# Soft-disc attention layer: norm-factor products in pairs, exponentials one step earlier, output units regrouped, value copies on VectorE

## The chip, the cores and the metric

One NeuronCore of a Trainium2 chip runs the whole program. The metric is device time in microseconds, the median of several executions. Engines are named as the profile names them: PE (matrix products), PEld (its weight loads), DVE (vector), ACT (activation functions), POOL (GpSimd), SP (which only issues DMAs here).

## The reference

Four layers act one after the other on a tensor of 8 images x 32 x 32 tokens x 256 channels in f32, each as `x = x + layer(groupnorm(x))`. The change lies in the last one, layer 3, a local attention with a soft disc as its window:

```
qkv = silu(x @ w_qkv.T);  q, k, v = split(qkv)                  # 8 heads of 32 channels
q, k = rope(rms_norm(q, w_qn)), rope(rms_norm(k, w_kn))         # norm over the 32 channels
wp = silu(x @ w_wp.T + b_wp);  width_raw, sharp_raw = split(wp) # one pair per token and head
width = sigmoid(width_raw) * sqrt(2) * 3 + 0.5
sharp = sigmoid(sharp_raw) * 9.5 + 0.5
mask = sigmoid((width - rel_dist) * sharp)                      # over the 7 x 7 neighbours
attn = softmax(scores / sqrt(32) - (1 - mask) * 10000)
out = rms_norm(attn @ v_window, w_on)                           # norm over all 256 channels
return silu((out + v) @ w_out.T)
```

The position that the rotary embedding sees is the head's, not the token's: q and k of a head are turned by the same angles, which cancel in the scores, so the kernel has no work for it.

## The kernel before, in words

Channels lie on the 128 partitions, in two chunks c of four heads each. Layer 3 works in 128 groups of 128 query tokens: image b (8), chunk c (2), pair of blocks t (8). A chunk number J = 2b + c stands for eight groups, so an image is 16 steps.

**The loop.** The order on PE, ACT, DVE and POOL is written by hand (`manual_schedule`): each engine executes what is emitted for it in exactly the order of emission, and waits at its head instruction for what this needs. SP is free of that order, but also works its own queue from the front. At step n the loop emits `scores(n+3)` (16 small products into four PSUM tiles `s`), `exps(n)` (four exponentials on ACT with row sums `su`), the planned units due at n, `logits(n+3)` (four reductions on DVE, which free the `s` tiles), the first half of `turn(n-2)` (transposes `pt` on PE, copied to `pts` by DVE), `finish()`, `soft(n+5)` (four tanh on ACT, the soft mask), `divide(n)` (reciprocal on DVE, multiply on POOL), the units due at n + 0.5, the second half of `turn(n-2)`, `finish()` again, `values(n-3)` (products `o`, copied into `oT` by DVE) and `masked(n+5)` (an addition on POOL).

**The units.** `Fillers` holds (due time, unit) pairs; those that are due are emitted in order of time, and of entry where times agree. A unit emits its products and often its ACT instruction at once and returns the rest (DVE, POOL, DMA) as a function, which goes into the list `later` and is emitted by the next `finish()`. For a chunk that starts at step n = 8J the plan has: `project` for k and q at n - 12 to n - 10.5 and for v at n - 7.5 and n - 7 (two products over 512 tokens, `qkv_ps`, L2015; a tanh `th`, L2000; the rest on DVE, with squares for q and k on POOL), `roots` at n - 8 (sums of squares by products into `ms_ps`, Ln and Exp on ACT, L2110 and L2111, which need another activation table and so a table load before and one after), four `head_scale` at n - 6 to n - 4.5 (a product of 32 rows with the norm factors, `fac_ps`, L2117, and a multiply on DVE, L2121), `in_strips` (POOL), and five `vturn` units (four transposes `vt` and a copy to `v` on ACT, L1744). Per image there are the group norm, `normed` (two ACT instructions), two `discs` units (products `wp_ps`, then a chain DVE, ACT, DVE, ACT, DVE that makes width and sharpness, L2055 to L2067), and the tail: squares of `oT`, a share in a later `roots`, four `tail_scale` (a product with the weights `won` on one row of factors, L2150, a multiply, an addition of v on POOL), and four `output` units (two products `out_ps` each, tanh, DVE, POOL, store) with a `reload` of the residual `xr` three steps ahead of each.

**Buffers.** All PSUM tiles come from one ring of eight banks, so a product can start only when the tile eight places back has been read. One step takes nine or ten of them. `xr` has three buffers, `su` four, `fac` two; the masks and probabilities live in nine fixed tiles.

**Where roots fall.** `roots` for J falls on step 8J - 8, that is on steps 0 and 8 of every image period of 16. In this text half A is the stretch from the roots at step 0 (odd J) to those at step 8, and half B the other. Images' tails come two images later: in steady state an output unit falls on steps 1.5, 7, 7.5 and 9.5, a tail product on steps 14 to 15.5.

Of the kernel before, what the change touches and what calls it, by code (L numbers as in the profile page):

```python
# [16 lines left out]
P = 128  # L17
# [15 lines left out]
def shape_constants():  # L33
# [55 lines left out]
    ).astype(f)  # L89
    k["k_spread"] = (p[:, None] % 32 == p[None] // 32).astype(f)  # L90
    return {n: np.ascontiguousarray(v) for n, v in k.items()}

# [13 lines left out]
def layouts(inputs):  # L106
# [38 lines left out]
    )  # L145
    a["l3_on"] = i["L3_conv_w_on"].reshape(2, P)
    a.update(shape_constants())
# [204 lines left out]
class First3(First):  # L352
# [8 lines left out]
    def early(self):  # L361
# [25 lines left out]
        def factors():  # L387
            won, spread = self.won, self.spread
            nc.vector.tensor_scalar(self.bwp, self.bwp, 0.5, None, ALU.mult)
            nc.gpsimd.tensor_scalar(self.wo, self.wo, 0.5, None, ALU.mult)  # L390
            nc.vector.tensor_mul(won[:, 0], won[:, 0], won[:, 1])
            nc.vector.scalar_tensor_tensor(
                spread[:, 0], won[:, 0], -(32.0**-0.5) / MASK_SCALE, spread[:, 0],
                ALU.mult, ALU.mult,
            )
            nc.vector.memset(won, 0.0)

        def weight():
            for h in range(2):
                nc.sync.dma_start(  # L400
                    self.won[32 * h + 8 : 32 * h + 9], a["l3_on"].unsqueeze(0)
                )

# [1230 lines left out]
class DiscStream(Stream):  # L1634
# [8 lines left out]
    def __init__(self, K, wk, cp, pp, pairs, n_img, ebufs):  # L1643
        super().__init__(K, wk, pp, pairs, n_img, ebufs)
        self.slots, self.s = 20, {}
        shape = [P, 4, 2 * self.PART]
        self.tiles = [cp.tile(shape, F32, name=f"e{i}") for i in range(ebufs)]
# [36 lines left out]
    def exps(self, n):  # L1684
        mx, e = self.mx.pop(n), self.prob(n)
        self.su = self.wk.tile([P, 4], F32, name="su", bufs=4)
        for j in range(4):
            self.nc.scalar.activation(  # L1688
                e[:, j], e[:, j], AF.Exp, scale=-1.0, bias=mx[:, j : j + 1],
                accum_out=self.su[:, j : j + 1],  # L1690
            )

    def divide(self, n):
        e = self.prob(n)
        self.nc.vector.reciprocal(self.su, self.su)  # L1695
        self.nc.gpsimd.tensor_mul(e, e, self.su.unsqueeze(2).to_broadcast([P, 4, NWIN]))  # L1696

# [37 lines left out]
    def value_unit(self, strips, dst, u):  # L1735
        ps = self.ring("vt")
        for i in range(4):
            col, r = divmod(4 * u + i, 5)
            self.nc.tensor.transpose(
                ps[: self.PART, i * P : i * P + P],  # L1740
                strips[:, col, 8 * r : 8 * r + 8].rearrange("p i j -> p (i j)"),
                self.K.ident,
            )
        self.nc.scalar.copy(  # L1744
            dst[: self.PART, 4 * u : 4 * u + 4, :],
            ps[: self.PART, :].rearrange("p (s c) -> p s c", c=P),
        )
# [202 lines left out]
def layer3(tc, K, src, dst, n_img, a, first):  # L1950
    nc = tc.nc
    pairs = disc_pairs()
    with tc.tile_pool(name="l3c", bufs=1, reuse_waits="tile") as cp, tc.tile_pool(
# [16 lines left out]
        K.ring = st.ring  # L1970
        bwp, sel, spread, won = first.bwp, first.sel, first.spread, first.won
        wo, win, eps = first.wo, first.win, first.eps
# [68 lines left out]
        def discs(b, u):  # L2041
# [11 lines left out]
            def rest():  # L2053
# [4 lines left out]
                )  # L2058
                th = wk.tile([P, 4, 16], F32, name="dth")
                nc.scalar.activation(th, d, AF.Tanh)  # L2060
                nc.vector.scalar_tensor_tensor(d, th, 1.0, d, ALU.add, ALU.mult)
                nc.scalar.activation(d, d, AF.Tanh, scale=0.5)
                wd, sp = d[:, :, 0:8], d[:, :, 8:16]
                md = math.sqrt(2.0) * 3
# [48 lines left out]

        def head_scale(J, s, h):
            g = slice(32 * (2 * s + h), 32 * (2 * s + h) + 32)
            ps = st.ring("fac_ps")
            nc.tensor.matmul(ps, spread[g, s], fac[J][g], start=True, stop=True)  # L2117

            def rest():
                d = dest(J, s, h)  # L2120
                nc.vector.tensor_mul(d, d, part(ps))  # L2121

            return rest
# [12 lines left out]
        def vturn(J, u):  # L2136
            b, c = divmod(J, 2)
            if u == 0:
                st.v[b, c] = wk.tile([P, st.slots, P], F32, name="v", bufs=2)
            st.value_unit(strips, st.v[b, c], u)  # L2140

# [4 lines left out]

        def tail_scale(J, b, c, h):
            g, hs = slice(32 * h, 32 * h + 32), slice(h * HALF, (h + 1) * HALF)
            ps = st.ring("fac_ps")
            nc.tensor.matmul(ps, won[g, c], fac[J][g], start=True, stop=True)  # L2150

            def rest():
                d = st.o[b, c][:, hs]
                nc.vector.tensor_mul(d, d, ps)
                nc.gpsimd.tensor_add(d, d, vT[b, c][:, hs])

# [28 lines left out]
        def plan_chunk(J):  # L2185
# [4 lines left out]
            for i in range(4):  # L2190
                s, h = 1 - i // 2, i % 2
                fill.add(n - 12 + i / 2, lambda s=s, h=h: project(J, s, h))
                fill.add(n - 6 + i / 2, lambda s=s, h=h: head_scale(J, s, h))
            fill.add(n - 7.5, lambda: project(J, 2, 0))
            fill.add(n - 7, lambda: project(J, 2, 1))
            fill.add(n - 6, lambda: in_strips(J))

        def plan_image(b):
            n = 16 * b
            if b:  # L2200
# [8 lines left out]
                for c in range(2):  # L2209
                    fill.add(n - 13.5 + c / 2, lambda c=c: normed(b, c))  # L2210
                for u in range(2):
                    fill.add(n - 10 + u / 2, lambda u=u: discs(b, u))
            for c in range(2):
                fill.add(n + 19 + c, lambda c=c: tail_sq(b, c))
                for h in range(2):
                    fill.add(
                        n + 30 + c + h / 2,
                        lambda c=c, h=h: tail_scale(2 * b + 4, b, c, h),
                    )
            for i in range(4):  # L2220
                at = n + 32 + (1.5, 7, 7.5, 9.5)[i]
                fill.add(at - 3, lambda i=i: reload(b, i // 2, i % 2))
                fill.add(at, lambda i=i: output(b, i // 2, i % 2))

        for J in range(2 * n_img + 3):
            b, c = divmod(J, 2)
            t = b - 2 if c == 0 and b >= 2 else None
            if J and (J < 2 * n_img or t is not None):
                fill.add(8 * J - 8, lambda J=J, t=t: roots(J, t))
            if J < 2 * n_img:  # L2230
                plan_chunk(J)
        for b in range(n_img):
# [14 lines left out]
        def finish():  # L2247
            while later:
                later.pop(0)()

        def start():

            units(-11)
            rest = [discs(0, 0), discs(0, 1), project(0, 1, 0)]
            rest[0]()
            rest[2]()
            r = project(0, 1, 1)
            rest[1]()
            r()
            soft(0)  # L2260
# [8 lines left out]
            in_strips(0)  # L2269
            for i in range(4):  # L2270
                head_scale(0, 1 - i // 2, i % 2)()
            masked(1)
# [6 lines left out]
        with tc.manual_schedule(engines={E.PE, E.Activation, E.DVE, E.Pool}):  # L2279
            start()  # L2280
            for n in range(-4, N + 3):
                if 0 <= n + 3 < N:
# [3 lines left out]
                    st.scores(n + 3)  # L2286
                if 0 <= n < N:
                    st.exps(n)
                units(n)
# [73 lines left out]
```

## Time and profile before

| | |
|---|---|
| median of three runs | 3330.1 us (3329.66 to 3331.37) |
| profiled execution | 3334.75 us, its span 3333.0 us |
| mean granted TensorE clock | 0.976 |
| busy share of the span | PE 96%, PEld 49%, DVE 66%, ACT 68%, POOL 45% |
| layer 3 | 2529 to 3333 us |
| transposes `pt` in it (L1706) | 1024 records, 164.7 us |
| projections `qkv_ps` (L2015) | 384 records, 191.4 us |
| norm-factor products (L2117) | 128 records, 81.7 us |
| tail products (L2150) | 64 records, 33.4 us |
| copies of v on ACT (L1744) | 80, 45.9 us |

The shares are means over four layers with different limits, so layer 3 has to be read from its own stretch. An f32 product of 512 columns shows as two records. Busy time is the time in which at least one instruction of the group was running; where records overlap, their mean duration times their number is more than that. The clock is what the throttle granted to PE, 1.00 being full speed.

### The profile page before, as it was taken

The numbers are of one execution on the slowest core, as the hardware profiler recorded it, in microseconds if no ns is written. First come the engines' busy times: TensorE is split into PE (matmuls) and PEld (weight loads), VectorE is DVE, ScalarE is ACT, GpSimd is POOL, SyncE is SP. The second block draws the span as 40 slices with busy tenths as digits, with TensorE's granted clock in tenths as the row PEclk, the third lists the DMA queues.
The fourth block names the chain that finished last, engine by engine and source line by source line (L and its number), as shares of the span: only waits on it lengthen the run. The fifth ranks groups of instructions, "written<-read, shape, count | busy, mean of one in ns | idle before, by whom it ended". The sixth has DMA issues, their size and how long they took to land. (4 is left out here: it accounts for less than half of the span.)

```text
span 3333.0 us, 77642 instructions
## 1 busy us (share of the span) xinstructions
PE 3203.6 (96%) x30792; PEld 1649.6 (49%) x30792; DVE 2185.0 (66%) x5570; ACT 2277.6 (68%) x5066; POOL 1491.7 (45%) x1073
## 2 busy tenths in 40 slices
PE   7999999999998999899999999999998999999997
PEld 3323323233232444667677766666664555555554
DVE  4776776777676667565555655666665667777775
ACT  3666666666676457755556547767676779888885
POOL 4233223323431011245444445344335658888777
PEclk9999999999999999999999999999998889999999
DMA  3000000000000666777787731111111001101001
GB/s 141 14 26 1 26 26 1 26 7 20 26 1 32 221 235 238 234 202 191 193 216 200 187 115 58 53 65 40 50 52 36 14 14 38 35 30 36 27 27 61
DMA packets 139183, 268.00 MB, mean 80 GB/s; under 512 B 9218, under 2 KB 77700, under 8 KB 130500
## 3 DMA queue, kind: packets, MB, share of 16 engines
q1 hardware_dynamic: 132436, 242.67, 24.3%
q10 hardware_dynamic: 6384, 20.37, 1.8%
q8 instruction: 243, 3.98, 0.5%
q14 instruction: 120, 0.98, 0.1%
HBM read 177.81 MB, written 85.20 MB: 79 GB/s over the span
## 5 line engine op out<-in xcount | busy, mean ns | idle before, releaser
L681 DVE TENSOR_TENSOR e<-s,ret 128x1024 f32<-128x1024 f32 x512 | 602.9, 1219 | 180.4 <-PE s L675 176.4
L685 ACT ACTIVATE ea<-e 128x1024 f32<-128x1024 f32 x512 | 535.1, 1055 | 267.8 <-DVE e L681 233.9
L675 PE MATMUL s<-qk,qk 32*128 32x512 f32 x2048 | 300.4, 640 | 2.4 <-POOL qk L567 1.7
L1564 POOL TENSOR_TENSOR e<-e,su 128x616 f32<-128x616 f32 (+2 forms) x128 | 157.3, 1229 | 269.8 <-DVE su L1563 240.2
L693 PE MATMUL sm<-ea,ones 128*32 128x512 f32 x2048 | 273.0, 604 | 2.0 <-DVE dn L701 2.0
L720 PE MATMUL num<-e,v 128*32 128x512 f32 x2048 | 266.6, 592 | 0.0
L1711 DVE COPY pts<-pt 112x512 f32<-112x512 f32 x256 | 175.9, 687 | 133.4 <-PE pt L1706 131.7
L2076 ACT ACTIVATE e<-win,disc 128x196 f32<-128x196 f32 x512 | 239.7, 544 | 0.3
L843 PE MATMUL up_ps<-x,wup 128*128 128x512 f32 x512 | 230.7, 605 | 3.2 <-POOL x L236 3.2
L1696 POOL TENSOR_TENSOR e<-e,su 128x784 f32<-128x784 f32 x128 | 191.3, 1495 | 82.7 <-DVE su L1695 53.9
L1688 ACT ACTIVATE e<-e,mx 128x196 f32<-128x196 f32 x512 | 228.0, 454 | 0.0
L2083 POOL TENSOR_TENSOR e<-e,win 128x784 f32<-128x784 f32 x128 | 201.7, 1576 | 37.8 <-issue 31.6
L1559 ACT ACTIVATE e<-e,mx 128x154 f32<-128x154 f32 (+2 forms) x512 | 212.3, 426 | 0.0
L1059 ACT ACTIVATE d<-d,cols 128x128 f32<-128x128 f32 x512 | 163.8, 392 | 67.9 <-POOL d L1050 67.8
L870 DVE SCALAR_TENSOR_TENSOR cv<-xm,par,cv 128x512 f32<-128x512 f32 x192 | 144.7, 754 | 85.5 <-ACT cv L865 80.9
L2015 PE MATMUL qkv_ps<-xq,w 128*128 128x512 f32 x384 | 191.4, 625 | 1.2 <-ACT fac L2110 1.2
L1255 POOL TENSOR_TENSOR decayed<-state,rb 128x520 f32<-128x520 f32 x48 | 50.8, 1058 | 304.7 <-PE sc L1188 112.5
L1796 PE MATMUL qkv_ps<-x,w 128*128 128x512 f32 x384 | 182.7, 613 | 1.6 <-POOL x L236 1.6
L1706 PEld LDWEIGHTS pt<-idg,e 128*112 128x112 f32 x1024 | 120.3, 139 | 120.5 <-issue 90.6
L675 PEld LDWEIGHTS s<-qk,qk 32*128 32x128 f32 x2048 | 85.3, 183 | 184.2 <-issue 120.4
L1706 PE MATMUL pt<-idg,e 128*112 128x128 f32 x1024 | 164.7, 287 | 8.4 <-DVE oT L1730 3.1
L1678 DVE CUSTOM_DVE_ANT_0 e<-s,e 128x196 f32<-128x196 f32 x512 | 153.7, 357 | 8.0 <-PE s L1665 4.2
(244 smaller groups left out, 6775.6 us busy)
## 6 DMA issues: line engine op xcount, KB each, us to landing
d<-l1rows SPq DMA_DIRECT2D x64, 512.0 KB
x<-x SPq DMA_DIRECT2D x25, 1024.0 KB
l1xm<-xm SPq DMA_DIRECT2D x16, 1024.0 KB
l1sz<-sz SPq DMA_DIRECT2D x16, 1024.0 KB
xv<-l1xm SPq DMA_DIRECT2D x32, 512.0 KB
l1xa<-xa SPq DMA_DIRECT2D x16, 1024.0 KB
xa<-l1xa SPq DMA_DIRECT2D x16, 1024.0 KB
rb<-l1rows SPq DMA_DIRECT2D x32, 512.0 KB
```

Source lines behind the costliest of these rows:

```text
L675: nc.tensor.matmul(s[:, j % 2], qk[b, 1, c][g, kb * P : (kb + 1) * P], qk[b, 0, c][g, h * HALF : (h + 1) * HALF], start=True, stop=True,)
L681: nc.vector.tensor_mul(e[n, i], s, m)
L685: nc.scalar.activation(ea[n, i], e[n, i], AF.Abs)
L693: nc.tensor.matmul(acc["sm"][g, :], ones, ea[n, j // 2][:, j % 2, :], start=kb == 0, stop=kb == 7,)
L720: nc.tensor.matmul(acc["num"][g, :], v[b][:, kb, vc], e[n, j // 2][:, j % 2, :], start=kb == 0, stop=kb == 7,)
L843: nc.tensor.matmul(ps, wup[:, kc, m * P : (m + 1) * P], seg(s)[:, kc], start=kc == 0, stop=kc == 1,)
L1559: self.nc.scalar.activation(p[:, j], p[:, j], AF.Exp, scale=-1.0, bias=mx[:, j : j + 1], accum_out=su[:, j : j + 1],)
L1688: self.nc.scalar.activation(e[:, j], e[:, j], AF.Exp, scale=-1.0, bias=mx[:, j : j + 1], accum_out=self.su[:, j : j + 1],)
L1706: self.nc.tensor.transpose(ps[: self.PART, at : at + P], self.tile(n)[:, 2 * i + j, k * self.PART : (k + 1) * self.PART], self.K.ident,)
L2015: nc.tensor.matmul(ps, w[:, kc, o : o + P], xq[b][:, kc, h * HALF : (h + 1) * HALF], start=kc == 0, stop=kc == 1,)
L2076: nc.scalar.activation(e[:, j], win[:, 0], AF.Tanh, scale=disc[b][:, i, 8 + h : 9 + h], bias=disc[b][:, i, h : h + 1],)
L2083: nc.gpsimd.tensor_add(e, e, win[:, 1].unsqueeze(1).to_broadcast([P, 4, NWIN]))
```

## The change

1. `head_scale` handles both token halves of q or of k in one unit: two products on two different groups of 32 rows stand next to each other on PE, with two PSUM tiles; the two multiplies follow together.
2. The tail's weight `w_on` moves out of the product: the product takes a matrix of ones on the factors' row, once for each token half instead of once for each half and channel chunk, and the weight, now a column per partition, is multiplied in by DVE in the same instruction as the factor.
3. `exps` is emitted one step earlier than `divide`, with `su` kept per group.
4. The copy of v out of PSUM is on DVE, in the next `finish()`, and no longer on ACT.
5. The chain of `discs` is cut into five pieces, one per `finish()`; `finish()` calls each function once and keeps what it returns for the next call.
6. The plan moves: v's two projections to n - 8.5 and n - 8 (the second is emitted just ahead of `roots`, which are entered later), `head_scale` to n - 6 and n - 5, `normed` from n - 13.5 to n - 15, `tail_scale` from n + 30 and later to n + 27.5 and n + 28.5 (n here an image's first step), the outputs from n + 33.5, 39, 39.5 and 41.5 to n + 29.5, 30.5, 31 and 31.5, in the order of token halves, with the reloads at n + 26.5 to n + 30.5.
7. Constants: a 128 x 128 matrix of ones on every row 8 of 32 is loaded in place of two rows of weights, and a memset before it goes.

```diff
         def weight():
-            for h in range(2):
-                nc.sync.dma_start(
-                    self.won[32 * h + 8 : 32 * h + 9], a["l3_on"].unsqueeze(0)
-                )
+            nc.sync.dma_start(self.won[:, 0], a["k_one8"])
+            nc.sync.dma_start(self.won[:, 1, 0:2], a["l3_on"])
...
-        self.nc.scalar.copy(
+        return lambda: self.nc.vector.tensor_copy(
             dst[: self.PART, 4 * u : 4 * u + 4, :],
...
-                th = wk.tile([P, 4, 16], F32, name="dth")
-                nc.scalar.activation(th, d, AF.Tanh)
+                return silu
+
+            def silu():
+                th = wk.tile([P, 4, 16], F32, name="dth", bufs=2)
+                nc.scalar.activation(th, disc[b][:, 4 * u : 4 * u + 4, :], AF.Tanh)
+                return lambda: silu2(th)
...
-        def head_scale(J, s, h):
-            g = slice(32 * (2 * s + h), 32 * (2 * s + h) + 32)
-            ps = st.ring("fac_ps")
-            nc.tensor.matmul(ps, spread[g, s], fac[J][g], start=True, stop=True)
+        def head_scale(J, s):
+            ps = [st.ring("fac_ps") for _ in range(2)]
+            for h in range(2):
+                g = slice(32 * (2 * s + h), 32 * (2 * s + h) + 32)
+                nc.tensor.matmul(ps[h], spread[g, s], fac[J][g], start=True, stop=True)
...
-        def tail_scale(J, b, c, h):
+        def tail_scale(J, b, h):
             g, hs = slice(32 * h, 32 * h + 32), slice(h * HALF, (h + 1) * HALF)
             ps = st.ring("fac_ps")
-            nc.tensor.matmul(ps, won[g, c], fac[J][g], start=True, stop=True)
+            nc.tensor.matmul(ps, ones[g], fac[J][g], start=True, stop=True)
 
             def rest():
-                d = st.o[b, c][:, hs]
-                nc.vector.tensor_mul(d, d, ps)
-                nc.gpsimd.tensor_add(d, d, vT[b, c][:, hs])
+                for c in range(2):
+                    d = st.o[b, c][:, hs]
+                    nc.vector.scalar_tensor_tensor(
+                        d, d, on[:, c : c + 1], ps, ALU.mult, ALU.mult
+                    )
+                    nc.gpsimd.tensor_add(d, d, vT[b, c][:, hs])
...
-                fill.add(n - 6 + i / 2, lambda s=s, h=h: head_scale(J, s, h))
-            fill.add(n - 7.5, lambda: project(J, 2, 0))
-            fill.add(n - 7, lambda: project(J, 2, 1))
+            for s in range(2):
+                fill.add(n - 5 - s, lambda s=s: head_scale(J, s))
+            fill.add(n - 8.5, lambda: project(J, 2, 0))
+            fill.add(n - 8, lambda: project(J, 2, 1))
...
-                    fill.add(n - 13.5 + c / 2, lambda c=c: normed(b, c))
+                    fill.add(max(n - 15, 2) + c / 2, lambda c=c: normed(b, c))
...
-                for h in range(2):
-                    fill.add(
-                        n + 30 + c + h / 2,
-                        lambda c=c, h=h: tail_scale(2 * b + 4, b, c, h),
-                    )
+                fill.add(n + 27.5 + c, lambda c=c: tail_scale(2 * b + 4, b, c))
             for i in range(4):
-                at = n + 32 + (1.5, 7, 7.5, 9.5)[i]
-                fill.add(at - 3, lambda i=i: reload(b, i // 2, i % 2))
-                fill.add(at, lambda i=i: output(b, i // 2, i % 2))
+                h, m = divmod(i, 2)
+                fill.add(n + (26.5, 27.5, 28, 30.5)[i], lambda h=h, m=m: reload(b, m, h))
+                fill.add(n + (29.5, 30.5, 31, 31.5)[i], lambda h=h, m=m: output(b, m, h))
...
         def finish():
-            while later:
-                later.pop(0)()
+            due = later[:]
+            later[:] = [r for r in [f() for f in due] if callable(r)]
...
-                if 0 <= n < N:
-                    st.exps(n)
+                if 0 <= n + 1 < N:
+                    st.exps(n + 1)
```

## The prediction

> **What bounds the kernel now.** I read the page's sums, then the busy time by stretches of layer 3 (the only layer that the change touches, apart from one memset and two loads at the end of layer 2). It runs from 2529 us to the end at 3333 us. Columns: stretch, length, then busy us (and instructions) of PE, weight loads, DVE, ACT, POOL; PE clock; DMA.
>
> ```profile
> PE 3203.6 (96%) x30792; PEld 1649.6 (49%) x30792; DVE 2185.0 (66%) x5570; ACT 2277.6 (68%) x5066; POOL 1491.7 (45%) x1073
> 2600.00:2700.00 100.00, 90.63 (x931) 51.24 (x930) 64.80 (x264) 79.48 (x230) 65.53 (x49) 0.86 0.04 12
> 2900.00:3000.00 100.00, 96.30 (x1033) 53.31 (x1032) 75.24 (x295) 89.72 (x258) 79.53 (x59) 1.00 0.12 36
> ```
>
> In the middle of the layer PE is the limit, with ACT close behind (90) and DVE and POOL under 80. Early, in 2600 to 2700, PE has less to do, stands idle 9 us and still has a clock of 0.86. So I asked for the chain and for PE in order of time, to price a product, and for the pieces around a roots step.
>
> ```profile
> 2872.66 1.05 PE fac_ps L2117 x2
> 2873.71 0.58 PE pt L1706 x4
> 2874.29 0.58 PE o L1722 x24
> 2874.87 0.52 PE s L1665 x16
> 303.20 1.14 PE L675 MATMUL s<-qk,qk 32*128 32x512 f32 x8
> L2150 PE MATMUL fac_ps<-fac,won 32*128 32x512 f32 x64 | 33.4, 636 | 0.0
> ```
>
> A product with the norm factors (32 rows, 128 columns, 512 tokens, two records) holds PE for 1.05 us by itself. The fifth line is layer 0: four products of exactly this shape on four different row groups, eight records, in 1.14 us. So row groups run side by side, and two neighbours cost what one does.
>
> The third view is the clock, in stretches of 3.413 us. That raster is mine: laid on the edges of the slow phases it gives 0.50 or 1.00 with hardly a value between, for the whole layer.
>
> ```profile
> 2676.56:2679.97 3.41, 3.24 (x17) 1.39 (x12) 3.41 (x17) 3.41 (x13) 3.01 (x3) 1.00 0.00 0
> 2679.97:2683.39 3.42, 3.42 (x44) 1.64 (x42) 2.94 (x14) 3.42 (x9) 3.36 (x5) 0.50 0.00 0
> 2690.21:2693.62 3.41, 3.41 (x5) 1.23 (x6) 1.22 (x8) 0.00 (x0) 1.30 (x1) 0.50 0.02 7
> 2693.62:2697.03 3.41, 3.41 (x45) 2.13 (x51) 2.08 (x6) 3.23 (x9) 1.37 (x2) 1.00 0.00 0
> 2673.30 0.75 DVE L2027 SCALAR_TENSOR_TENSOR vT<-th,qkv_ps 128x256 f32<-128x256 f32 x2 [5.29 <-ACT th L2000]
> ```
>
> PE was half-clocked for four such stretches from 2679.97, just after the thin steps behind a roots step. The last line says why PE was starved there: DVE stood 5.29 us on a tanh queued on ACT behind the roots (two table loads of 1.28 us, Ln 0.69, Exp 0.63: 3.9 us). Such a four-stretch phase takes 13.65 x 0.5 = 6.8 us of PE work away. Layer 3 has four of these, one of six stretches, and three single ones.
>
> Last, the halves of an image, from Ln to Ln.
>
> ```profile
> 2569.11 0.69 ACT L2110 ACTIVATE fac<-ms_ps,eps 128x512 f32<-128x512 f32 x1
> 2768.28 0.69 ACT L2110 ACTIVATE fac<-ms_ps,eps 128x512 f32<-128x512 f32 x1
> 2860.94 0.69 ACT L2110 ACTIVATE fac<-ms_ps,eps 128x512 f32<-128x512 f32 x1
> 2908.53 0.69 ACT L2110 ACTIVATE fac<-ms_ps,eps 128x512 f32<-128x512 f32 x1
> 2952.07 0.69 ACT L2110 ACTIVATE fac<-ms_ps,eps 128x512 f32<-128x512 f32 x1
> ```
>
> A full image takes 47.6 + 43.5 = 91.1 us. The four early halves (2569.11 to 2768.28), which have next to no output work, take 49.8 each: with less work they are longer.
>
> **Part by part.**
>
> *Products.* 32 pairs; two lie in the lead-in where PE waits on others, 30 save about 1.05 - 0.1 = 0.95 us: 29 us. The tail needs one product per half and not one per half and channel chunk: 16 fewer x 1.05 = 17 us. If pairs did not run side by side, only the 17 would be left. On DVE nothing goes: two multiplies of 0.68 us per pair stay, and the tail's multiply by the weight column has the shape of the layer's other 512-wide scalar_tensor_tensor (0.68).
>
> Against this the Trainium skill has a rule ("TensorEngine Tiling (Array Packing)", section PSUM Bottleneck): tiling speeds up TensorE but not the emptying of PSUM. By it alone a pair would still take DVE's 2 x 0.6 us and half of the 29 us would be lost; the row of DVE at 75 of 100 says that there is room in a full image.
>
> *PE per full image.* Base per step (s 0.52, o 0.58, two pt at 0.45 to 0.58): about 2.05, so 16.4 per half. Half A (after the odd roots): 16.4, six projections at 1.8, three outputs at 1.8, four products 4.2, five vt 2.5, discs 3.8, roots 2.8: 46 before. After: no outputs, two pairs 2.2: 38.5. Half B before: 16.4 + 10.8 + 1.8 + 4.2 + 4.2 (tail) + 2.5 + 1.1 = 41. After, with all four outputs: 42.3. Sum 87 to 81.
>
> *ACT.* exps 1.78 and soft 1.78 per step, 28.5 per half; roots 3.9; tanh 0.48 each (nine in half A and seven in B before, six and ten after); normed 2.3 and discs 0.9 in A; v copies 0.47 each, five per half before. Half A 42.2 before, 38.5 after; half B 38.1 and 37.2. The ten v copies of an image go to DVE at the 0.6 net of a pts copy: DVE from 75% of 91 = 68 to 74 us.
>
> *Waits that go.* Exps a step ahead: the reciprocal on DVE (behind it the second pts copy, then oT, then PE's ring of eight banks) no longer needs ACT in the same step. v's second half is projected ahead of the roots and no output follows them, so the 5.29 us wait has no cause; the next tanh that DVE waits for is four steps on. The disc chain (27 us of ACT and DVE waiting in 16 units) is spread over five finishes.
>
> *Waits that come.* In half A steps 1 to 3 have 9 us of PE work against 13 us of ACT; PE can run a good step ahead until logits want soft, and then waits for ACT. POOL in steps 2 to 5 (each divide 1.5 and masked 1.58, plus strips 1.7, squares 1.9 and 1.06) has 22 us against PE's 18: covered by the two steps between masked and logits, and costing about 1 us where that runs out. In half B, DVE has 15 us in steps 9 to 11 (statistics, pairs, tail) against PE's 10. What is late next after a roots step is therefore ACT, then POOL, then DVE. xr has three buffers: the fourth reload waits for the first store, behind it on SP stand only stores; some 11 us of path against 14 us until its add. Zero, or 1 us per image on POOL if late. normed moves 1.5 steps up, still behind its last reader. The weight loads in layer 2 are 64 KB behind 20 us of other work: zero; the memset that goes is off the path too.
>
> *Sum.* Before, a full image stood 4.4 us over its larger engine sums (46 + 41). After: 38.5 + 42.3 + 4.4 = 85 at best, 89 if the new waits come to 8; I take 87. Five images (2768 to 3231, 462.5 us) give 5 x 87 = 435, plus three half-clock phases, 20: 455, a gain of 7; with one phase 20. I take 10. Early halves: ACT is the larger, 38.5 + 35.3 = 74 per image, with 4 to 10 over it 78 to 84, so 156 to 168 for 199.2; four phases at 6.8, partly in PE's spare time, give up to 27 back: gain 4 to 43, I take 20. End: image 6's outputs move from behind the last group into the thin steps; between ms_ps (3308.3) and the first tail add (3314.3) one output goes, 2.4 us, and one POOL add of 1.27 ahead of the squares; with the thinner last halves 5. Lead-in 0, plus or minus 3. Together 35: from the profiled 3334.75 (span 3333.0 and 1.75 around it) to 3299.8. The profiled run is 4.65 above the median of the runs, so 3295.
>
> **The clock, and a rule on it.** The row: half clock begins after a stretch in which PE was busy 3.24 of 3.41 us, in the steps of small products and transposes, and lasts one or four stretches. The Trainium skill ("TensorE: Matmul & The Clock Gate", Part 1) gives windows of 3413 ns, as here, but has the clock fall after an idle window. By that rule the changed kernel, which has no such gap, would lose nothing, and the time would be about 3275; by the row the thin steps are enough.
>
> **Rivals.**
> *All of it is collected* (0.15): 46 us of products and some 15 of lost clock, 3262 to 3279. For: PE at 97%. Against: ACT's sum equals PE's in half A.
> *Given back* (0.18): stalls after the roots grow by what PE was spared; 3312 to 3337. For: the early halves, which have PE sums like the new half A and take 50 us. Against: they have the th wait that goes.
> *Slower by the clock* (0.12): three thin steps and not two behind each roots step put every half into a four-stretch phase: 15 x 6.8 = 102, less the 43 lost now (25 stretches), is +59, against the 46 of products: about 3343. It decides from some 13 of 15 halves on; below that the products win.
>
> **How the numbers follow.** The forecast (3279 to 3312) has 0.55, with median 3295. 0.2% is 6.7 us, about what a measurement of this kernel can tell from no change: faster is below 3323, and takes in the first two cases and 0.10 of the third, 0.80; same 0.08; slower 0.12. The range 3264 to 3326 leaves out the clock case, the upper part of the third and the tip of the first.
>
> **What would show it.** Right: fac_ps pairs with 4 records in about 1.1 us; 32 records of the ones product in place of 64; no DVE wait of 5 us on th; halves near 43 and 44. Wrong: halves A at 47 or more with PE idle on ACT; half-clock stretches in most halves; pairs at 2.1 us; POOL waiting for xr from a DMA.

## The result, and the profile after

The change makes the kernel faster, by a fifth of the 35 us that were forecast: median 3324.27 us (20 runs, 3310.87 to 3328.11) against 3331.55 (20 runs, 3327.07 to 3337.76), ratio 0.9968 [0.9958, 0.9978]. The runs of after spread over 17 us, and the time goes with the mean clock: 3311 to 3314 at 0.974 to 0.976, 3325 to 3328 at 0.970 to 0.972. The profiled execution is one of the latter: 3327.51 us, span 3325.3, clock 0.971 (before 3334.75, 3333.0 and 0.976).

The page's sums and the same two stretches as before:

```profile
PE 3200.6 (96%) x30760; PEld 1664.1 (50%) x30760; DVE 2220.2 (67%) x5649; ACT 2240.7 (67%) x4986; POOL 1491.4 (45%) x1073
2600.00:2700.00 100.00, 96.50 (x1085) 58.39 (x1083) 78.40 (x309) 84.57 (x250) 72.79 (x54) 0.93 0.04 12
2900.00:3000.00 100.00, 95.71 (x992) 54.83 (x992) 76.71 (x292) 79.40 (x233) 75.61 (x56) 0.91 0.11 33
```

PE has 32 records less and is busy only 3 us less. In the early stretch it is fuller (96.5 for 90.6) at a better clock. In the middle of the layer, which had run at 1.00, the clock is now 0.91. The halves of an image from Ln to Ln show where:

```profile
2853.31 0.69 ACT L2125 ACTIVATE fac<-ms_ps,eps 128x512 f32<-128x512 f32 x1
2895.63 0.69 ACT L2125 ACTIVATE fac<-ms_ps,eps 128x512 f32<-128x512 f32 x1 [0.75 <-PE ms_ps L2117]
2950.46 0.69 ACT L2125 ACTIVATE fac<-ms_ps,eps 128x512 f32<-128x512 f32 x1
2853.31:2895.63 42.32, 40.48 (x478) 24.55 (x478) 32.24 (x129) 38.31 (x112) 33.49 (x24) 1.00 0.11 33
2895.63:2950.46 54.83, 53.21 (x480) 28.99 (x484) 41.65 (x149) 38.23 (x112) 40.53 (x31) 0.84 0.11 35
```

Half A takes 42.3 us at full clock (forecast near 43, before 47.6); half B takes 54.8 at 0.84 (forecast near 44, before 43.5). The raster of 3.413 us in that half B, and PE in order of time (start, length, then the operation):

```profile
2898.54:2901.96 3.42, 1.97 (x33) 1.29 (x32) 3.35 (x16) 3.42 (x13) 2.65 (x2) 1.00 0.00 0
2901.96:2905.37 3.41, 3.41 (x19) 1.59 (x16) 3.41 (x12) 3.41 (x13) 2.35 (x3) 0.50 0.00 0
2915.61:2919.02 3.41, 3.41 (x45) 2.15 (x45) 2.97 (x8) 0.00 (x0) 2.52 (x2) 0.50 0.00 0
2919.02:2922.44 3.42, 3.42 (x12) 1.52 (x10) 2.25 (x12) 1.75 (x4) 3.00 (x3) 1.00 0.00 0
...
2901.47 1.79 PE L1664 MATMUL s<-kp,qT 32*64 32x196 f32 x16 [0.38 <-DVE mx L1677]
2903.18 3.06 PE L2134 MATMUL fac_ps<-fac,spread 32*128 32x512 f32 x4
2909.96 2.08 PE L2134 MATMUL fac_ps<-fac,spread 32*128 32x512 f32 x4
```

In steps 8 and 9 PE waits in small pieces for DVE, which is busy 3.35 of 3.42 us (0.5 us for `pts`, 0.5 for `oT`, 0.4 for `mx`), and works 1.97 of 3.42 us. The next five stretches run at half clock, through PE work that has no gap; a pair of products takes 2.1 to 3.1 us there. Five such stretches take 8.5 us of PE work. Every half B but the last two has four or five of them: in the ten halves after the early four (2755 to 3234 here, 2768 to 3231 in before) 21 stretches are half-clocked, in before 5. Two of the 21 stand alone, in halves A that took 42.3 us all the same; the other 19 lie in half B.

Set against the forecast, by profiled runs:

| | before | after | forecast gain | measured gain |
|---|---|---|---|---|
| lead-in half, to the second Ln | 23.7 | 27.8 | 0 | -4.1 |
| early four halves | 199.2 | 183.0 | 20 | 16.2 |
| the next ten halves | 462.5 | 479.2 | 10 | -16.7 |
| last two halves, end, first Ln | | | 5 | 12.3 |

Everything but the ten halves came within 8 us of its forecast; these were 27 us worse, all of it in half B.

### The profile page after: what moved, and what is told of

It is laid out like the page before. It is cut to its first block, busy times and chain, and to the rows that moved or that the text cites. A ratio compares the mean times of both kernels' runs of the same rounds, so it can differ in the third digit from the quotient of the medians.

```text
span 3325.3 us, 77702 instructions
## 1 busy us (share of the span) xinstructions
PE 3200.6 (96%) x30760; PEld 1664.1 (50%) x30760; DVE 2220.2 (67%) x5649; ACT 2240.7 (67%) x4986; POOL 1491.4 (45%) x1073
## 5 line engine op out<-in xcount | busy, mean ns | idle before, releaser
L1254 POOL TENSOR_TENSOR decayed<-state,rb 128x520 f32<-128x520 f32 x48 | 50.8, 1058 | 306.7 <-PE sc L1187 80.1
```

## The experiments

Two theories to begin with. *Clock*: the thin steps 8 to 11 of half B drop the clock, and that is what took the gain. *Give-back*: VectorE and ScalarE set half B whatever the clock. "Clock loss" below is the sum of (1 - granted clock) over 2530 to 3310 us of the profiled run: 44.8 us in before, 66.2 in after. Ratios are to before. An idle product is one of constants into the PSUM tile that the real product behind it then overwrites.

### Idle products in the thin steps, or the statistics later

**e1_fill**: two idle products of 128 rows and 512 columns in front of each pair and of the last turn of values, six per half B.

```diff
             ps = [st.ring("fac_ps") for _ in range(2)]
+            if J % 2 == 0 and J > 0:
+                burn(ps[0], 2)     # 2 x matmul(ps, K.ident, wo, start=True, stop=True)
...
+            if u == 4 and c:
+                st.before_vt = lambda ps: burn(ps, 2)
```

> The changed kernel with six idle products more in each half B: full-array products of constants (128 rows, 128 columns, 512 tokens) put ahead of the v transposes of step 9 and of the pairs of steps 10 and 11, two each, into banks that the real product then overwrites. They add about 6 x 0.9 = 5.4 us of PE work to each half B and remove nothing. Clock theory (the thin steps 9 to 11 let the clock fall to 0.50, and that costs 7 to 8 us in each half B): full clock in half B, halves of 48 to 50 us in place of 54 to 56, kernel 15 to 35 us FASTER than the changed one, about 3290 to 3310. Give-back theory (the waits on DVE, ACT and POOL set half B, and the slow clock only fills time in which PE would wait): halves B as long or longer, kernel 0 to 35 us slower than the changed one, 3325 to 3360.

Measured 3304.32 us, 0.9902 [0.9886, 0.9917], clock loss 20.0: 20 us faster than after, by added work that nobody needs. Two idle products take 1.98 us, and the pair behind them takes what the prediction priced:

```profile
2889.25 1.98 PE L2134 MATMUL fac_ps<-wo,idg 128*128 128x512 f32 x4
2891.17 1.13 PE L2145 MATMUL fac_ps<-fac,spread 32*128 32x512 f32 x4
2881.96:2933.00 51.04, 50.80 (x492) 27.42 (x496) 41.26 (x149) 38.22 (x111) 40.39 (x31) 1.00 0.11 33
```

Half B is 51.0 at full clock, with some 6 us of idle work in it. The clock theory holds here, and give-back, which asked for a slower kernel, falls as the main cause.

**e2_stats**: the next image's statistics, mean and root later, so that DVE is freer in steps 8 to 10.

```diff
-                        max(n - 23.5, -3) + i / 2,
+                        max(n - 19.5, -3) + i / 2,
-                fill.add(max(n - 21, -1), lambda: gn.mean(b, later))
-                fill.add(max(n - 19, 1), lambda: gn.root(b, later))
+                fill.add(max(n - 17.5, -1), lambda: gn.mean(b, later))
+                fill.add(max(n - 16.5, 1), lambda: gn.root(b, later))
```

> The changed kernel with the group-norm statistics of the next image four steps later (from steps 8.5 to 10 to steps 12.5 to 14, its mean and root moved with them), out of the stretch in which DVE has 15 us of work against PE's 10. It moves 2.5 us of DVE work per image and changes nothing on PE or ACT. Give-back theory: DVE is what half B waits for in steps 9 to 11, so each half B loses 2 to 3 us, the kernel 10 to 18. Clock theory: PE waits less at 8.5 to 10, so the clock falls less often; where it does not fall 7 to 8 us more are gained per half, the kernel 10 to 45 faster in all, with fewer stretches of 0.50. If neither holds (ACT sets these steps): within 5 us of the changed kernel.

Measured 3303.55 us, 0.9905 [0.9886, 0.9923], clock loss 38.4. Taking away PE's waits works as well as filling them. The two halves B that kept their clock took 47.8 us: that is half B's length at full clock, with the statistics moved; the forecast had it near 44.

### Undoing parts of the change

**e3_single**: `head_scale` again one product per unit, four per half, at n - 6 to n - 4.5.

> The changed kernel with the norm-factor products single again, four units at n - 6 to n - 4.5 as before the change; all else stays changed. By the sum of the prediction it loses the pairs' 29 us: about 3350. Clock theory: two more products of 1.05 us in each of the thin steps cost PE nothing while it waits there and keep the clock up more often: 3315 to 3335, with fewer stretches of 0.50 in half B. Give-back theory: the pairs sit in steps that PE waits in anyway, so single ones cost nothing: within 8 us of the changed kernel, with as many slow stretches.

Measured 3349.35 us, 1.0037 [1.0022, 1.0051], clock loss 94.4. The clock theory missed: single products do not hold the clock better. The loss is 25 us over after, with 28 us more of clock loss, so this run does not say what a pair is worth by itself.

**e4_oldplan**: outputs, reloads and tail products at their old steps.

> The changed kernel with the tail products at n + 30 and n + 31 and the outputs and reloads at the steps of before (1.5, 7, 7.5, 9.5 of the period); pairs, exps ahead, v copies on DVE and the ones product stay. Half A gets three outputs back (5.4 us of PE), half B keeps one, in step 9. Clock theory: step 9 is no longer thin, half B runs at full clock more often, and is 40 to 46 us; half A 45 to 48; kernel about 3285 to 3315. Give-back theory: outputs behind the roots bring their tanh behind the table loads again and DVE waits for it: half A 47 or more, half B 46 or more at any clock, kernel 3320 to 3335.

Measured 3341.47 us, 1.0026 [1.0014, 1.0038], clock loss 79.4; outside both expectations. Half A is back at 50 to 53 us, half B at 44 to 48. The regrouped outputs are worth 17 us on this base. Half A's clock was 0.87 to 0.93 there, two to four half-clock stretches in each, and the 3.4 to 6.8 us of PE work that these take away cover what half A has over before's 47.6.

**e9_exps**: `st.exps(n)` in place of `st.exps(n + 1)`.

> The exponentials of a group again in the group's own step, in front of its reciprocal; all else as after. Theory of the prediction: the reciprocal on VectorE then waits for ScalarE in the same step again, with the transposes' copies behind it: waits of TensorE on pts, oT and su grow by 0.5 to 1 us in the thin steps, and these make more half-clock stretches: 3330 to 3350, clock loss 70 to 95. Rival (the two steps of slack elsewhere are enough, the move is worth nothing): 3316 to 3330, clock loss 55 to 70.

Measured 3337.12 us, 1.0010 [0.9999, 1.0021], clock loss 87.6: 13 us slower than after, as the prediction's mechanism had it. PE waits 14.8 us for `pts` in front of the pairs' products; in after it waits there only for the factors, once, 2.0 us.

**e10_vcopy**: `nc.scalar.copy` in place of `nc.vector.tensor_copy`, at the same place.

> The copies of the turned values (0.68 us each on VectorE) go back to ScalarE, at the same place of the order; all else as after. If VectorE's queue in steps 8 to 10 of half B makes the steps thin for TensorE: one copy fewer there, B shorter by 1 to 4 us, 3300 to 3318, clock loss 45 to 60. If ScalarE behind the roots is what is late next (as the prediction had it): half A from 42.3 to 44 or more, 3330 to 3350. If both have room: 3318 to 3330.

Measured 3328.11 us, 0.9989 [0.9973, 1.0005], clock loss 74.2; half A 42.8 to 44.4. A loss of 4 us by the medians, 7 by the ratios; the intervals overlap.

### What holds the clock

**e5_stats_disc**: e2_stats, and the second disc piece (eight products that are needed anyway) from step 6.5 to step 9.5.

```diff
-                    fill.add(n - 10 + u / 2, lambda u=u: discs(b, u))
+                    fill.add(n - (10, 6.5)[u], lambda u=u: discs(b, u))
```

> As e2_stats (statistics, mean and root of the next image four steps later), and the eight products of the second disc piece, real work of TensorE on full arrays, moved from step 6.5 of the image's second half-plan to step 9.5, into the thin steps; nothing is added. Clock theory (the loss is whole stretches of 3.413 us at half clock, set off by thin TensorE work in steps 8 to 11 of half B): the moved products do what the idle ones of e1_fill did, for nothing; the clock loss falls from e2_stats' 38 us to 15 to 30, and the time to 3280 to 3298. Give-back theory (VectorE and ScalarE set these steps, whatever the clock): the disc piece's own VectorE and ScalarE work now lies in the same steps, and the time is e2_stats' 3303.6 plus 3 to 12.

Measured 3289.29 us, 0.9862 [0.9841, 0.9883], clock loss 24.8: 35 us faster than after, with the same work.

**e6_stats_fill1**: e2_stats with half of the idle products.

> As e2_stats, with half of the idle products of e1_fill (three per half B: one in front of each pair of norm-factor products and one in front of the last turn of values). Clock theory: two edits that each took away part of the loss (66 to 20 by the idle products, 66 to 38 by the later statistics) leave 10 to 20 together; half B falls to 46 to 49 at full clock, and seven halves B save 2 to 5 us each over e1_fill: 3270 to 3292. Give-back theory: the idle products cost their own time, some 0.49 us each, 21 of them, on top of e2_stats: 3308 to 3316. If three are too few to hold the clock: 3298 to 3306, the clock loss 30 to 40.

Measured 3289.85 us, 0.9869 [0.9849, 0.9889], clock loss 12.8; five full halves B take 48.7 us, with about 3 us of idle products in each, and none has a half-clock phase of four or five stretches.

**e7_fill32**: e1_fill with idle products of 32 rows (`K.ident[g], wo[g]`).

> As e1_fill, the same number of idle products at the same places, but of 32 rows instead of 128 (rows 0 to 31, or those of the product behind them). TensorE is busy for as long as in e1_fill by the profile. If the clock goes by TensorE's busy time, the time is e1_fill's: 3300 to 3309, clock loss 18 to 30. If it goes by how much of the array works, a quarter of the rows counts for little: the half-clock phases stay, clock loss 50 to 80, and the time is that of after or above it, 3318 to 3345. Give-back theory: after plus the products' time, 3335 to 3350.

Measured 3314.97 us, 0.9934 [0.9915, 0.9952], clock loss 30.6: between the two expectations. Three halves B are as long as e1_fill's (50.7 to 50.8), three others have two or three half-clock stretches. A quarter of the rows holds the clock most of the time, not always.

**e8_fill_dense**: the same six idle products per half B in steps 12 and 13, in front of the projections.

> Control of e1_fill: the same number of idle full-array products per half B (six), but in the dense steps 12 and 13, in front of the projections of the next half. Clock theory, place matters: the thin steps 8 to 11 stay thin, the phases stay (clock loss 50 to 75), and 42 products of some 0.49 us stand in steps that TensorE itself bounds: 3324 plus 10 to 21, so 3334 to 3346. If it is only the amount of work that counts (a mean over the image): as e1_fill, 3300 to 3312. If it is only chance of phase (any shift of the order changes where the stretches fall): anything between 3305 and 3335, with a clock loss between 20 and 50.

Measured 3364.20 us, 1.0085 [1.0062, 1.0109], clock loss 57.8. The expectation's 0.49 us per idle product was wrong: the row of e1_fill shows two in 1.98 us, so 42 cost 41.6, and 3324 + 41.6 is 3366. With that price the control is plain: in the dense steps the products cost nearly all of their time and hold little of the clock (loss 57.8 against 66.2); in the thin ones they pay for themselves.

**e12_before_fill**: idle products in before, eight in each of the early halves.

> The kernel before, with idle full-array products (of constants, into the bank that the real product then overwrites) in the early halves J 1 to 5: two in front of each product of v with the projection weights and two in front of the first of each pair of norm-factor steps, eight per half, 40 in all, where TensorE waits or is half-clocked. Clock theory: the phases of before at 2574, 2632, 2680 and 2731 (18 stretches, some 30 us of TensorE's work, partly in its spare time) go or shrink, the clock loss falls from 45 to 15 to 30: 3305 to 3325. If the early halves are set by ScalarE and VectorE whatever the clock: 3328 to 3336. If the products only add their 0.49 us: up to 3354.

Measured 3330.30 us (12 runs), 0.9994 [0.9979, 1.0009], clock loss 10.4. The phases went, as the clock theory said, but 40 idle products are 40 us by the corrected price, and by the ratio the time fell by 2. The time lies in the band of the second expectation (3328 to 3336), so it does not decide against that one. The early four halves of the profiled run went from 199.2 to 188.7 us. What the early phases had cost by themselves is not separated by this run.

**e15_disc_only**: after with the disc piece alone moved.

> After with the second disc piece alone moved to step 9.5; the statistics, mean and root stay where after has them. If eight real products in the thin steps are what holds the clock: 3288 to 3300, clock loss 20 to 35. If the statistics on VectorE in steps 8 to 10 must go too: 3303 to 3322, half B 50 to 55 in some images.

Measured 3295.93 us, 0.9892 [0.9877, 0.9906], clock loss 35.2. Real products in the thin steps do most of what e5_stats_disc does; its half B is 50 to 52 us where e5_stats_disc has 48.2, so the statistics have a share too.

### What the parts are worth with the clock held

With e5_stats_disc the full halves run at 1.00 nearly throughout, and the parts can be priced against it. A full image by engine in before, in e5_stats_disc and in e11_disc_single (half A, then half B; columns as above):

```profile
2860.94:2908.53 47.59, 45.15 (x494) 26.02 (x493) 33.60 (x132) 42.39 (x120) 38.65 (x29) 1.00 0.15 46
2908.53:2952.07 43.54, 43.49 (x466) 23.56 (x465) 35.71 (x136) 38.53 (x112) 35.34 (x28) 1.00 0.08 26
```
```profile
2834.40:2875.84 41.44, 39.35 (x462) 22.96 (x462) 32.55 (x127) 38.16 (x111) 33.53 (x24) 1.00 0.11 34
2875.84:2923.99 48.15, 47.05 (x496) 26.97 (x500) 42.29 (x151) 38.26 (x113) 40.50 (x31) 1.00 0.13 40
```
```profile
2745.77:2787.20 41.43, 39.48 (x462) 22.55 (x462) 32.52 (x127) 38.16 (x111) 33.49 (x24) 1.00 0.11 34
2787.20:2835.90 48.70, 47.92 (x496) 26.87 (x500) 42.36 (x151) 38.26 (x113) 40.41 (x31) 1.00 0.13 39
```

**e11_disc_single**: e5_stats_disc with single products as in e3_single.

> e5_stats_disc with the norm-factor products single again: the worth of the pairs with the clock held. By the prediction's price (0.95 us for each of 30 pairs): e5 plus 28, 3312 to 3322, at a clock loss no more than 8 above e5's 24.8. By the busy time of the lines (a half's four single products 4.5 us before, its two pairs 2.8 to 3.4 in e5, so 0.55 to 0.85 per pair): e5 plus 15 to 25, 3302 to 3314. If what e3_single lost was clock alone (its loss is 28 above after's, its time 25): e5 plus 0 to 8 where the clock stays held, or, where single products make the thin steps thinner and set the phases off again, e5 plus 15 to 45 with the clock loss up by as much.

Measured 3291.14 us, 0.9877 [0.9855, 0.9898], clock loss 28.2. By the medians 1.9 us over e5_stats_disc, by the ratios 5; the intervals overlap. The prediction's 29 us for the pairs are not there. The windows say why: half A is 41.4 either way, since PE has 2 us to spare in it (one half A of e11_disc_single, at a clock of 0.85, took 44.5); in half B a pair saves 0.3 us and not 0.95. PE and its weight loads in order of time, e11_disc_single and then e5_stats_disc:

```profile
2799.53 0.69 PE L2132 MATMUL fac_ps<-fac,spread 32*128 32x512 f32 x1
2799.54 0.69 PE L2166 MATMUL fac_ps<-fac,won 32*128 32x512 f32 x1
```
```profile
2885.35 1.63 PE L2134 MATMUL fac_ps<-fac,spread 32*128 32x512 f32 x4
2885.86 0.29 PEld L2134 LDWEIGHTS fac_ps<-fac,spread 32*128 32x128 f32 x2 [0.22 <-DVE kp L2139]
2886.91 0.65 PE L1705 MATMUL pt<-idg,e 128*112 128x128 f32 x4
2887.49 1.12 PE L2169 MATMUL fac_ps<-fac,won 32*128 32x512 f32 x2
```

The last single product stands next to the tail's product, on other rows, and the two run side by side already. With pairs the tail's product is alone again, and the second pair takes 1.63 us, because its second product starts late: the weight load stood 0.22 us for DVE's multiply by the factors (`kp`). In after itself it is the same. Of the 17 pairs behind the lead-in that ran wholly at full clock there, one took 1.13 us; the 16 others took 1.69 or 1.72, like these two of half A:

```profile
2857.30 1.69 PE L2134 MATMUL fac_ps<-fac,spread 32*128 32x512 f32 x4
2857.87 0.29 PEld L2134 LDWEIGHTS fac_ps<-fac,spread 32*128 32x128 f32 x2 [0.31 <-DVE pts L1710]
2862.00 1.72 PE L2134 MATMUL fac_ps<-fac,spread 32*128 32x512 f32 x4
2862.60 0.29 PEld L2134 LDWEIGHTS fac_ps<-fac,spread 32*128 32x128 f32 x2 [0.30 <-DVE kp L2139]
```

A pair needs two tiles of the ring at once, and here DVE had not read the second one yet. That the wait is for this tile is inferred from the releaser that the profile names; it was not tested.

**e14_disc_tail**: e5_stats_disc with the tail's product made once per channel chunk again.

> e5_stats_disc with the tail's product made twice per half again, once for each channel chunk, one behind the other on the same rows (16 products more, as before the change); VectorE's and GpSimd's work unchanged. By the prediction's price (1.05 us each, half B set by TensorE: 47.05 of 48.15 us busy): e5 plus 13 to 18. If half of it is hidden in the waits of half B (1.1 us per half) and at the ends: e5 plus 6 to 12. If products in the thin steps are free, as the single ones of e11_disc_single nearly were: e5 plus 0 to 4.

Measured 3293.04 us, 0.9884 [0.9869, 0.9898], clock loss 24.0: by the medians 3.8 us over e5_stats_disc, by the ratios 7; half B 49.5 where it kept its clock, that is 1.3 more for two products of 1.05; three others, with one half-clock stretch each, took 50.6 to 50.7. The prediction had 17.

**e13_disc_exps**: e5_stats_disc with `st.exps(n)`.

> e5_stats_disc with the exponentials of a group in the group's own step, as before the change: what their move is worth with the clock held. On after it was 13 us (e9_exps, with 21 us more of clock loss). If that was the clock alone: e5 plus 0 to 5 at a clock loss within 8 of e5's 24.8. If it is the wait (reciprocal behind ScalarE, pairs behind the transposes' copies, 14.8 us of TensorE waiting on pts in e9_exps): e5 plus 10 to 25, half A 42 to 47, clock loss up to 40.

Measured 3301.85 us, 0.9907 [0.9890, 0.9923], clock loss 55.6: 12.6 us over e5_stats_disc by the medians, 15 by the ratios. PE's waits in layer 3 (total, times, longest):

```profile
PE fac_ps L2134 <- DVE pts L1710: 14.6, 7, 2.3
PE fac_ps L2134 <- DVE disc L2055: 6.8, 7, 1.8
```

The wait in front of the pairs is back, and the clock loss with it, 55.6 where both expectations had it at 40 or less. It is half A that pays: three of its five full ones have three or four half-clock stretches and take 43.7 to 45.2 us, while half B keeps its clock and is 0.6 us longer. By these halves most of what the exponentials' move is worth comes through the clock. Of the parts priced here it is worth the most.

**e16_disc_vcopy**: e5_stats_disc with the copies of v on ScalarE.

> e5_stats_disc with the copies of the turned values back on ScalarE. On after this was 0 to 4 us slower (e10_vcopy). VectorE has 42.3 us of work in half B's 48.15, ScalarE 38.3: half B 0 to 1 us shorter, half A (ScalarE 38.2 of 41.4) 0 to 2 longer, so e5 minus 3 to plus 10. By the prediction (ScalarE is what is late next in half A): plus 5 to 10.

Measured 3282.12 us, 0.9854 [0.9839, 0.9869], clock loss 26.6, the lowest median of all and below both expectations, though its interval overlaps that of e5_stats_disc. Half B is 47.3, half A 41.2, the last two halves 5 us longer. So this part of the change is worth nothing or a little less with the clock held. The version beats both kernels by 42 us (after) and 48 us (before, in the same session).

## Why the prediction was right and wrong

**Right.** The sign, though 3324 lies outside the forecast's 3279 to 3312; half A (42.3 for "near 43"), which runs at the sum of PE and small waits; 32 records of the ones product (22.0 us) for 64 (33.4); the early halves (16 for 20), where the half-clock stretches went from 19 to 11. The exponentials a step ahead act by the chain named (reciprocal, `pts`, PE's ring), 13 us on both bases. And the wait on `th` behind the roots: VectorE had waited for it at v's projections 17 times in layer 3 of before, 46.9 us, and does so three times now. Part of it has gone to k's (VectorE's waits in layer 3, total, times, longest; the first line is before, the others after):

```profile
DVE vT L2027 <- ACT th L2000: 46.9, 17, 6.1
DVE kp L2027 <- ACT th L2000: 24.1, 15, 4.0
DVE vT L2027 <- ACT th L2000: 5.1, 3, 2.9
```

**Wrong: the clock term of the ten halves.** "Three half-clock phases, 20" was three phases in five images; there were six, of 1, 5, 5, 5, 1 and 4 stretches. The two single ones, in half A, cost no length. The four long ones cost 29.6 us: these halves B took 56.0, 54.8, 55.7 and 54.3 us, where e2_stats had 47.8 at full clock. The prediction had the mechanism, and told it as a rival, but only as a case of nearly all halves, placed behind every roots step. Here the long phases came in half B alone: after the even roots DVE has statistics, disc pieces, pairs and the tail at once. The prediction counted that as "DVE has 15 us in steps 9 to 11 against PE's 10" and priced it as a wait of a few us; its real price was the half clock that follows the wait.

**Wrong: the base of a full image.** "I take 87" was 42.3 + 47.8 = 90.1 at full clock (half B as in e2_stats), five times 3.1 or 15.6 us. PE's work fell from 88.6 us (45.15 + 43.49) to 86.4 in e5_stats_disc, 2.2 and not the 6 of the sum ("87 to 81"). The term that was mis-sized is the products': 29 us for the pairs measured 2 to 5 with the clock held, 17 for the tail's measured 4 to 7. "Two neighbours cost what one does" held in the few pairs of 1.13 us; the others, at full clock, took 1.63 to 1.72, their second product waiting for DVE. The prediction had weighed such a loss, half of the 29, and set it aside because DVE was busy 75 of 100. Part of the gap could be seen in before: the sum gives PE 41 us in half B, where the row has 43.5.

**How the two add up.** Five images of 90.1 are 450.6; the ten halves took 479.2, so the clock cost 28.6 (the fifth half B, 46.9, was 0.9 shorter than 47.8) where the sum had 20. Base 15.6 and clock 8.6 make the 24 us by which the ten halves exceed the sum's 455. This takes e2_stats' half B as that of after with its clock held.

**The end and the lead-in** missed by +7 and -4 us. In the lead-in the clock is 0.82, in before 0.93; e14_disc_tail, with the same lead-in, had it at 0.93 and took 25.0 us, so some 2.8 of the 4.1 go with the clock. Of the 12.3 at the end, the last two halves gave 9.1; why they gave more than forecast stays open.

**Smaller slips of the prediction.** Layer 3 of before has four single half-clock stretches, and a phase of two at its end, where it counts three single ones. An image of 91.1 stands 4.1 us over 46 + 41, not 4.4. Neither moves the forecast.

**The Trainium skill's rule** ("TensorE: Matmul & The Clock Gate", Part 1) has the clock fall after an idle window. One phase in layer 3 of before fits it: the six stretches from 2574.16 follow one with PE busy 0.00 of 3.42 us. In the five images no stretch was idle; the clock fell after one with PE busy 1.97 of 3.42 us, and in before (at 2676.56) after 3.24 of 3.41. Taken as the prediction took it, the rule left the changed kernel near 3275, by the prediction's estimate; the row, by which thin steps are enough, held. With the clock held, e5_stats_disc and e16_disc_vcopy stand at 3289 and 3282; they hold it by further edits, so they are not a measure of the 3275.

**The other rivals.** "Given back" had the time (3312 to 3337) but not the reason: the halves with PE sums like the early ones, A, ran at 42.3 us, and behind the even roots PE stands idle only 1.6 us of half B's 54.8. "All of it is collected" fell with the price of the pairs and with the clock.

**What stays open**: what the clock counts. Idle products in thin steps hold it, the same in dense steps hardly do; 32 rows hold it mostly (clock loss 30.6, with 128 rows 20.0); the raster names no bound on busy time, since in after stretches with 2.5 and even 1.93 of 3.4 us (at 2871.24) passed with no fall behind them and one with 3.24 (in before) was the last ahead of a fall. Parts of the change that were not undone alone, above all the disc chain over five `finish()` calls and v's projection ahead of the roots, are not priced; that they carry the early gain is argued, not shown.

## What to carry to other kernels

Thin stretches on TensorE cost twice in this kernel: the wait itself, and often four to five stretches of 3.4 us at half clock behind it. So before saving TensorE work in a thin place, lay the clock's raster over the steps, and move real work (here eight products of a disc piece, by one line of the plan: 28 us) from dense steps into the thin ones. Price a saved product only where TensorE bounds the half it stands in, and look at its neighbours: a product on other rows next to it may run beside it already, and two that need two PSUM tiles at once may have to wait for the second.

## What was not expected of the hardware

Useless work made the kernel faster: 44 idle products, 43.6 us of TensorE's time, took 20 us off (e1_fill), and about as many a few steps later added 40 (e8_fill_dense). The half-clock phases are whole stretches of 3.413 us, one to six at a time, never a part, and outlast their cause: the last of the five at 2915.61 to 2919.02 had PE busy all of its 3.41 us. At half clock a pair took 2.08 us (after, at 2909.96); at full clock it took 1.13 where its second product did not wait (e1_fill, at 2891.17).
